# Layer 1's own rows scattered in rank order at layer 0's end, layer 3's masks built in batch norm's stage, and three chunks' sums on ScalarE

## The chip, the cores and the metric

The kernel runs on one core of one Trainium2 chip. The metric is the device time of one execution in microseconds (us). The program computes four layers of a small graph network in one launch. A core has five engines that work through queues of their own: PE (TensorE, the matrix array), DVE (VectorE), ACT (ScalarE), POOL (GpSimd) and SP (SyncE, which in this kernel only issues transfers). Semaphores order them against each other. POOL also issues all transfers whose addresses come from an index in memory (gathers and scatters)[...].

## The reference

There are N = 2708 nodes with D = 128 features, and an adjacency matrix `adj` of 2708 x 2708 floats that is stored densely but has about 17 non-zeros in a row, the diagonal always among them. Each layer is wrapped in the same way:

```python
x = _layernorm(x + layer(x, adj), axis=-1)      # four times
# layer 0
msg = H.T @ X ; msg * (1 / H.sum(axis=0))[:, None]
# layer 1
s = x @ msg_w[:, :D].T ; d = x @ msg_w[:, D:].T
messages = gelu(s[:, None, :] + d[None, :, :] + msg_b)
aggregated = einsum('ijd,ij->id', messages, adj)
h = gelu(concatenate([x, aggregated]) @ upd_w.T + upd_b) + x ; layernorm(h)
# layer 2
h = A @ (x @ W) + b ; batch norm of h over the nodes ; leaky relu, 0.2
# layer 3, for each of 4 heads
E = leaky_relu((x @ w1)[:, None, :] + (x @ w2)[None, :, :], 0.01)
s = exp(tanh(E @ a / 8) * 8) * A ; s = s / s.sum(-1)
out = leaky_relu(s @ x @ Wlin.T, 0.01)           # then the four heads side by side @ w
```

Layers 1 and 3 need the messages only where `adj` is not zero, so the kernel first finds each row's non-zeros.

## The kernel before

**Blocks and ranks.** The nodes are handled in 22 blocks (21 of 128 nodes and one of 20). The blocks form two groups, `GROUPS` = (0, 13), (13, 22), split at `SPLIT` = 13. Within each group the nodes get a `rank` by their number of non-zeros, largest first, and from layer 1 on a block means 128 nodes that are neighbours in rank. So all rows of a block have nearly the same count, and block b needs only `CAPS[b]` messages per row (30 down to 8). `perm` holds for each rank the node's own number, `idx` the numbers of its neighbours, `ls` their weights.

**Layer 0 and the search (0 to about 205 us).** SP loads row blocks of `adj` through a ring of nine buffers (L388). For each block, `count_and_sum` lets PE add the block's part of `adj.T @ x` and of the column sums to PSUM (L405), POOL clears the diagonal (L395) and ScalarE counts the row's non-zeros with a Sign over the whole row (L416). `extract` (L420 to L471) is VectorE's search: the eight largest of each of 11 segments of 247 columns with their places, then the 32 largest of these as two sets of keys, one for the value and one for the place. `ranking(g)` (L478 to L504) sends the counts of a group to all partitions by way of DRAM and lets ScalarE count, with one Sign for each block (L502), how many keys lie above; `ranked(g)` turns the count into `rank`. `lists` (L514 to L543) decodes the keys on VectorE into weights and column numbers, and `place` scatters each row's list on POOL to its rank in `lists_dram`; `sorted_lists` (L558) reads the table back in rank order into `ls`, `idx` and `perm`. In this stage only the first group, blocks 0 to 12, is searched; group 1's ranking is issued after layer 0's last block, and its search takes place inside layer 1. The order of VectorE's instructions here is that of the program; the other engines' queues are ordered by a scheduler from the program's dependencies.

**Layer 0's end (175 to 205 us).** `layer0` (L722 to L783) is a generator that normalises up to four blocks at once: the sum and residual on VectorE, Squares and a root on ScalarE, the scaling on VectorE into `xs`, a transposition and the product with `wd_t` on PE (that is d), a copy on ScalarE. Both halves go to `dx_dram` in node order through SP: d in the row's first 512 bytes, x in the second. Six of these generators run staggered (L785 to L795). The weights that PE needs transposed come in through `weight` (L369), whose load ScalarE issues and whose transposition is at the front of PE's queue.

**Layer 1 with layer 2 (205 to 840 us).** A loop over the 22 rank blocks in the order `TURNS`. For a block, `own_row` gathers its own 1-KB rows (d and x) from `dx_dram` by `perm` on POOL into one of three buffers `x_s`, one block ahead (L808). `messages` computes s on PE, then gathers chunks of up to eight neighbours' d, one gather of 128 rows of 512 bytes for each neighbour place, into five buffers `msg` (L816; `dx_dram` is seen as a table of 2N half rows, hence the factor 2 in `idx`); VectorE adds s, ScalarE takes gelu, VectorE weighs and sums. Beside it, two at most of the row blocks are loaded again and transposed through PE into `at_dram` (`transposed`, L898), and group 1's search is done. `update` (L860) makes the new x of the block, scatters it, and keeps x @ W. From the twelfth block on, `layer2(k)` (L942) gathers 128 rows of `at_dram` at a time (1.35 MB) on POOL into the same ring and multiplies them on PE (L949) while layer 1 still runs.

**Batch norm (840 to 905 us).** Statistics over the nodes, the normalised x, its products with the second weights of layer 3 (the rows of `t2_dram`), and scatters of x by rank.

**Layer 3 (905 to 1610 us).** The nodes of each group are cut once more, into 24 blocks of `BLOCKS3`: a block takes g rows in each quarter of the partitions with up to 128 // g neighbours each, and consists of chunks of four rows each; 100 chunks in all. `masks(g)` (L1164) builds for each of the seven values of g, on first use, constant 0/1 matrices that copy, sum and pick rows; it is called inside `prepare`, step by step, while the preceding block is at work. The order of PE, VectorE and ScalarE is that of the program here. For each chunk: `fetch` gathers the neighbours' four parts from `t2_dram` on POOL into one of nine buffers; `repeated` (L1275) copies x1 to the neighbours' partitions on PE, into z3 (three rows) and z1 (one row, where PE adds the neighbours' part too, L1288); VectorE adds z3 to the gathered rows (L1483). Then the score of each row and head, a sum over 128 numbers, is done in one of two ways: `scores` (L1294) does product and sum on VectorE, four instructions a row, and `products` (L1303) with `sums_of_products` (L1310) does the product of two rows in one VectorE instruction and the sums in eight ScalarE instructions. Of each chunk's four rows, two take the first way and two the second. `rest` and `finish` (L1319, L1368) do tanh, exp, the weights, the products with the neighbours' x (L1360), the heads' linear maps (`al`, `lin` at L1386), the last product and the normalisation; `step` queues their pieces between the chunks' instructions. A dense version of the last two layers behind a flag is not run with these inputs.

Of the kernel before, what the change touches and what calls it, by code (L numbers as in the profile page):

```python
# [9 lines left out]
FP = mybir.dt.float32  # L10
AF = mybir.ActivationFunctionType
ALU = mybir.AluOpType
# [73 lines left out]
def gnn_resnorm_kernel(  # L86
# [124 lines left out]

    dx_dram = tables.tile([NBLK * P, 2 * D], FP, name="dx_dram")
# [30 lines left out]
    def gather(dst, table, index, rows=N):  # L243
        nc.gpsimd.indirect_dma_start(  # L244
            out=dst,
            out_offset=None,
            in_=table[0:rows, :],
            in_offset=bass.IndirectOffsetOnAxis(ap=index, axis=0),
        )
# [84 lines left out]
    with ExitStack() as layer:  # L334
# [22 lines left out]
        nc.gpsimd.iota(places_i, pattern=[[-256, CAND]], base=256 * CAND, channel_multiplier=0)  # L357
# [11 lines left out]
        def weight(src, name):  # L369
            raw = small.tile([P, P], FP, name="raw_w")  # L370
            nc.scalar.dma_start(raw, src)
# [142 lines left out]
        def lists(b0, b1):  # L514
# [8 lines left out]
            nc.vector.tensor_copy(rows[:, :, 2 * SLOTS], cnt[:, b0:b1])  # L523
            nc.vector.tensor_copy(rows[:, :, 2 * SLOTS + 1], node[:, b0:b1])
            nc.vector.tensor_copy(rows[:, :, 0], diag[:, b0:b1])
            nc.vector.tensor_copy(rows[:, :, SLOTS], node[:, b0:b1])
            nc.vector.tensor_copy(code, k2[:, b0:b1, 0 : SLOTS - 1])
            nc.vector.tensor_scalar(low, code, 255, None, ALU.bitwise_and)
            nc.vector.tensor_scalar(seg, code, 8, None, ALU.arith_shift_right)
            nc.vector.tensor_scalar(seg, seg, -1.0, float(CAND), ALU.mult, ALU.add)  # L530
            nc.vector.tensor_scalar(seg, seg, 3, None, ALU.arith_shift_right)
            nc.vector.tensor_scalar(seg, seg, float(NSEG - 1), 0.0, ALU.min, ALU.max)
            cols = rows[:, :, SLOTS + 1 : 2 * SLOTS]
            nc.vector.scalar_tensor_tensor(cols, seg, float(SEGW), low, ALU.mult, ALU.add)
            nc.vector.tensor_scalar(cols, cols, float(N - 1), 0.0, ALU.min, ALU.max)
            nc.vector.scalar_tensor_tensor(cols, v1, 0.0, cols, ALU.is_gt, ALU.mult)
            nc.vector.tensor_scalar(
                seg, seg, float(SPAN), float(127 - TOP), ALU.mult, ALU.add
# [19 lines left out]
        def sorted_lists(g):  # L558
# [3 lines left out]
            for c0, c1, n in parts:  # L562
# [6 lines left out]
                nc.vector.tensor_scalar(  # L569
                    idx[0:n, c0:c1, :], ls[0:n, c0:c1, SLOTS : 2 * SLOTS], 2.0, None, ALU.mult  # L570
                )
# [150 lines left out]
        def layer0(b0, count, n):  # L722
# [31 lines left out]
            nc.vector.reciprocal(v, v)  # L754
            for j in range(count):
                nc.vector.tensor_scalar(
                    xs[0:n, b0 + j, :], h[0:n, j, :], sums[:, j : j + 1], v[:, j : j + 1],
# [3 lines left out]
            nc.sync.dma_start(  # L761
                dx_dram[b0 * P : b0 * P + w, D : 2 * D].rearrange("(b p) w -> p b w", p=n),
# [1259 lines left out]
```

## Time and profile before

| | |
|---|---|
| time, median of 3 runs | 1965.46 us |
| the three runs | 1963.5, 1975.81, 1965.46 us |
| the profiled execution | 1612.16 us |
| its span on the core | 1610.4 us |
| its mean TensorE clock | 0.708 of full speed |
| PE, PE weight loads | 1170.0, 827.4 us (73%, 51%) |
| VectorE, ScalarE, POOL | 1182.0, 697.6, 897.8 us (73%, 43%, 56%) |
| moved by DMA | 288.21 MB, mean 179 GB/s |
| message gathers (L244), 368 | 349.7 us, 950 ns each |
| layer 3's gathers (L244), 400 | 403.6 us, 1009 ns each |
| ScalarE's sums (L1314), 800 | 235.2 us, 295 ns each |
| VectorE's scores (L1298), 400 of each kind | 91.7 us, 284 ns each (z1's row) |
| VectorE's products (L1306), 100 | 121.1 us, 1211 ns each |
| VectorE's sum with z3 (L1483), 100 | 174.8 us, 1748 ns each |

The profile covers one execution. Its span is the time from the first to the last instruction on the core; busy times are of that span. A row of the profile names line, engine, operation and the tiles it writes and reads; "idle before" is the engine's idle time ahead of such an instruction, with what ended it. PE's clock is the share of full speed that the chip granted. The profiled execution is far shorter than the timed runs, so times taken from it are compared with each other and not with the median.

### The profile page before, as it was taken

Reading aid. Unit: us, or ns where it says so; the run is one execution under the profiler, and the core shown is the slowest. Engines: PE = TensorE matmul, PEld = TensorE weight load, DVE = VectorE, ACT = ScalarE, POOL = GpSimd, SP = SyncE. Lnnn points to the kernel's source line nnn. Section 1 sums busy time; section 2 is a strip of 40 time slices with the busy share of each in tenths; the row PEclk is TensorE's granted clock in tenths of the full one; section 3 lists DMA queues with packets and bytes.
Section 4 is the critical chain, followed back from the end, with each engine's and each line's share of the span. In section 5 each row is a group of like instructions: output and inputs, shape, how many; then the busy total and the mean of one; then the engine's idle time right before and its main releaser. Section 6 shows DMA issues by size and latency. Waiting matters only on the chain. (4 is left out here: it accounts for less than half of the span.)

```text
span 1610.4 us, 23528 instructions
## 1 busy us (share of the span) xinstructions
PE 1170.0 (73%) x5771; PEld 827.4 (51%) x5771; DVE 1182.0 (73%) x5376; ACT 697.6 (43%) x2670; POOL 897.8 (56%) x996
## 2 busy tenths in 40 slices
PE   6996333555357536666896689988888988998994
PEld 6896323344246435565783234544554545555553
DVE  7999967888356554444547398897888888888883
ACT  3448467655235311111115244544444555455442
POOL 1001167777667577765613577665656656676521
PEclk9898655655556677677678766776787778767675
DMA  8733368888358734343333779875766766877630
GB/s 273 286 141 127 94 186 201 246 248 237 101 136 215 224 77 164 128 169 140 104 109 121 245 229 225 234 223 159 221 204 198 209 187 166 230 199 215 186 92 8
DMA packets 164685, 288.21 MB, mean 179 GB/s; under 512 B 46610, under 2 KB 118512, under 8 KB 157439
## 3 DMA queue, kind: packets, MB, share of 16 engines
q0 software_dynamic: 60496, 190.76, 40.9%
q1 hardware_dynamic: 95923, 90.91, 18.1%
q10 hardware_dynamic: 8120, 4.95, 1.2%
q8 instruction: 48, 0.79, 0.2%
q14 instruction: 98, 0.80, 0.2%
HBM read 242.50 MB, written 43.97 MB: 178 GB/s over the span
## 5 line engine op out<-in xcount | busy, mean ns | idle before, releaser
L244 POOL DMA_INDIRECT g<-t_dram,idx x400 | 403.6, 1009 | 189.3 <-issue 141.1
L244 POOL DMA_INDIRECT msg<-dx_dram,idx x368 | 349.7, 950 | 119.1 <-issue 93.9
L1314 ACT ACTIVATE sum_junk<-g 126x128 bf16<-126x128 f32 (+3 forms) x800 | 235.2, 295 | 115.8 <-DVE g L1306 63.4
L1283 PE MATMUL z<-x,copies 32*126 32x512 f32 (+3 forms) x800 | 210.8, 875 | 33.1 <-DVE g L1483 32.3
L949 PE MATMUL acc<-x_nat,at_rows 128*128 128x128 f32 (+2 forms) x968 | 151.0, 319 | 83.1 <-DMA at_rows<-at_dram,perm 82.7
L923 PE MATMUL pt_a<-ident,rows 128*128 128x128 f32 (+2 forms) x475 | 110.1, 388 | 133.6 <-ACT at_sb L928 132.3
L949 PEld LDWEIGHTS acc<-x_nat,at_rows 128*128 128x128 f32 (+2 forms) x968 | 138.0, 226 | 93.2 <-DMA at_rows<-at_dram,perm 75.9
L1483 DVE TENSOR_TENSOR g<-g,z 126x1536 f32<-126x1536 f32 (+3 forms) x100 | 174.8, 1748 | 11.7 <-PE z L1283 11.2
L1288 PE MATMUL z<-g,ident 126*126 126x512 f32 (+3 forms) x200 | 164.7, 918 | 0.0
L923 PEld LDWEIGHTS pt_a<-ident,rows 128*128 128x128 f32 (+2 forms) x475 | 80.2, 200 | 156.4 <-ACT at_sb L928 152.6
L1314 ACT ACTIVATION_READ_ACCUMULATOR sum_junk<-g 126x1 f32 (+3 forms) x800 | 149.5, 187 | 0.0
L835 DVE SCALAR_TENSOR_TENSOR own<-msg,ls,own 128x128 f32<-128x128 f32 (+1 forms) x302 | 105.4, 349 | 56.1 <-ACT msg L853 53.5
L1360 PEld LDWEIGHTS po_s<-wm,g 126*128 126x128 f32 (+3 forms) x800 | 118.6, 232 | 42.1 <-DVE wm L1347 32.7
L1360 PE MATMUL po_s<-wm,g 126*128 126x24 f32 (+6 forms) x800 | 120.5, 305 | 25.0 <-DVE wm L1347 23.3
L405 PE MATMUL acc<-x_nat,rows 128*128 128x129 f32 (+3 forms) x1012 | 130.5, 291 | 11.2 <-DMA rows<-in_adj_dram 11.2
L405 PEld LDWEIGHTS acc<-x_nat,rows 128*128 128x128 f32 (+2 forms) x1012 | 125.2, 201 | 16.2 <-DMA rows<-in_adj_dram 11.7
L1306 DVE SCALAR_TENSOR_TENSOR g<-g,a_ps 126x1024 f32<-126x1024 f32 (+3 forms) x100 | 121.1, 1211 | 0.0
L435 DVE MAX8 cv<-rows 128x8 f32<-128x247 f32 (+2 forms) x242 | 95.5, 400 | 6.7 <-POOL rows L395 6.7
L1288 PEld LDWEIGHTS z<-g,ident 126*126 126x126 f32 (+3 forms) x200 | 40.6, 254 | 116.3 <-issue 89.7
L1283 PEld LDWEIGHTS z<-x,copies 32*126 32x126 f32 (+3 forms) x800 | 63.7, 239 | 70.6 <-DVE g L1483 27.0
L430 DVE FIND_INDEX8 ci<-cv,rows 128x8 uint32<-128x247 f32 (+2 forms) x242 | 98.4, 407 | 0.0
L1298 DVE SCALAR_TENSOR_TENSOR g<-z,a 126x128 f32<-126x128 f32 (+3 forms) x400 | 91.7, 284 | 2.3 <-PE z L1288 0.9
(297 smaller groups left out, 2093.2 us busy)
## 6 DMA issues: line engine op xcount, KB each, us to landing
rows<-in_adj_dram SPq DMA_DIRECT2D x34, 1354.0 KB
at_dram<-at_sb SPq DMA_DIRECT2D x105, 256.0 KB
g<-t_dram,idx POOLq DMA_INDIRECT x400
msg<-dx_dram,idx POOLq DMA_INDIRECT x368
t_dram<-t_row SPq DMA_DIRECT2D x21, 256.0 KB
at_dram<-at_sb SPq DMA_DIRECT2D x21, 64.0 KB
dx_dram<-x_nat SPq DMA_DIRECT2D x5, 256.0 KB
dx_dram<-d_sb SPq DMA_DIRECT2D x5, 256.0 KB
```

The source lines that it names most:

```text
L244: nc.gpsimd.indirect_dma_start(out=dst, out_offset=None, in_=table[0:rows, :], in_offset=bass.IndirectOffsetOnAxis(ap=index, axis=0),)
L405: nc.tensor.matmul(accs0[k][0:m, c0 : c0 + f1 - f0], lhsT=rows[0:n, j0 : j0 + m], rhs=x_nat[0:n, b, f0:f1], start=k not in started, stop=( ...
L430: nc.vector.max_index(out=ci[0:n, at], in_max=cv[0:n, at], in_values=rows[0:n, c0 : c0 + cw])
L835: nc.vector.scalar_tensor_tensor(to, m, v, last, ALU.mult, ALU.add)
L923: nc.tensor.transpose(pt[0:m, j, 0:n], rows[0:n, c0 : c0 + m], ident[0:n, 0:n])
L949: nc.tensor.matmul(accs2[ib // 4][0:m, (ib % 4) * D : (ib % 4 + 1) * D], lhsT=at[0:n, i0 : i0 + m], rhs=xw[0:n, b, :], start=(k == 0 and i ...
L1283: nc.tensor.matmul(z3[0:e, r, :] if r < 3 else z1[0:e], lhsT=copies[g][rows, j, :], rhs=own[b][1][rows, :], start=True, stop=r < 3, skip_g ...
L1288: nc.tensor.matmul(z1[0:e], lhsT=ident[0:e, 0:e], rhs=g4[0:e, 3, 0:HD], start=False, stop=True, skip_group_check=True,)
L1306: nc.vector.scalar_tensor_tensor(z, z, 0.0, a_ps[0:e].unsqueeze(1).to_broadcast((e, 2, HD)), ALU.max, ALU.mult)
L1314: nc.scalar.activation(junk[0:e], g4[0:e, r, hd * D : (hd + 1) * D], AF.Identity, accum_out=sc[0:e, r, hd : hd + 1],)
L1360: nc.tensor.matmul(po[:, p0 * HEADS : (p0 + g) * HEADS], lhsT=g4s[i][0:e, r, HD : HD + D], rhs=wm[0:e, 4 * i + r, :, :], start=True, stop= ...
L1483: nc.vector.tensor_tensor(z, z, z3[0:e], ALU.add)
```

## The change

It has six pieces.

- **The tables of layer 0's end.** d gets a table of its own, `d_dram`, in node order, so that the messages' gathers read rows of it by the node's number without the factor 2. d and x of a block lie side by side in a new tile `dx`, and POOL scatters each block's 1-KB rows to their rank in `dx_dram`: 22 scatters.
- **Own rows.** `own_row` becomes a plain load of 128 neighbouring rows of `dx_dram` on SP's queue, in place of the gather on POOL.
- **The ranking of group 1** has to be there before its blocks are scattered: it is issued ahead of layer 0's loop, and `ranked(1)` comes after the first loop instead of inside layer 1. Blocks from the 13th on wait in their generator until then.
- **Weights and lists.** `weight` loads on SP's queue instead of ScalarE's. `lists` decodes the segment in three operations fewer on VectorE, and four of its copies go to ScalarE.
- **Masks.** `masks` is no longer a generator and moves to batch norm's stage: the kinds 4, 5 and 6 ahead of the loop that normalises, the other four behind it. The results live in a pool of their own, `ready`.
- **Three rows' sums.** In every even chunk of a block of layer 3, three rows instead of two take the way over `products` and ScalarE's sums, and VectorE's four `scores` for the third row are left out. Odd chunks stay as they were.

The diff, cut to its core:

```diff
+    d_dram = tables.tile([NBLK * P, D], FP, name="d_dram")
     dx_dram = tables.tile([NBLK * P, 2 * D], FP, name="dx_dram")
...
-        nc.gpsimd.iota(places_i, pattern=[[-256, CAND]], base=256 * CAND, channel_multiplier=0)
+        nc.gpsimd.iota(places_i, pattern=[[-256, CAND]], base=256 * (CAND + 7), channel_multiplier=0)
...
             raw = small.tile([P, P], FP, name="raw_w")
-            nc.scalar.dma_start(raw, src)
+            nc.sync.dma_start(raw, src)
...
-            nc.vector.tensor_copy(rows[:, :, 2 * SLOTS], cnt[:, b0:b1])
-            nc.vector.tensor_copy(rows[:, :, 2 * SLOTS + 1], node[:, b0:b1])
-            nc.vector.tensor_copy(rows[:, :, 0], diag[:, b0:b1])
-            nc.vector.tensor_copy(rows[:, :, SLOTS], node[:, b0:b1])
+            for at, of in ((0, diag), (SLOTS, node), (2 * SLOTS, cnt), (2 * SLOTS + 1, node)):
+                nc.scalar.copy(rows[:, :, at], of[:, b0:b1])
...
-            nc.vector.tensor_scalar(seg, code, 8, None, ALU.arith_shift_right)
-            nc.vector.tensor_scalar(seg, seg, -1.0, float(CAND), ALU.mult, ALU.add)
-            nc.vector.tensor_scalar(seg, seg, 3, None, ALU.arith_shift_right)
-            nc.vector.tensor_scalar(seg, seg, float(NSEG - 1), 0.0, ALU.min, ALU.max)
+            nc.vector.tensor_scalar(seg, code, 11, None, ALU.arith_shift_right)
...
-                nc.vector.tensor_scalar(
-                    idx[0:n, c0:c1, :], ls[0:n, c0:c1, SLOTS : 2 * SLOTS], 2.0, None, ALU.mult
-                )
+                nc.vector.tensor_copy(idx[0:n, c0:c1, :], ls[0:n, c0:c1, SLOTS : 2 * SLOTS])
...
+            dx = brief.tile([P, count, 2, D], FP, name=f"dx{count}", bufs=3 if count > 1 else 2)
...
-            d_sb = brief.tile([P, 4, D], FP, name="d_sb")
-            nc.scalar.copy(d_sb[0:n, 0:count], pm[0:n, 0:count])
+            nc.scalar.copy(dx[0:n, :, 0, :], pm[0:n, 0:count])
             nc.sync.dma_start(
-                dx_dram[b0 * P : b0 * P + w, 0:D].rearrange("(b p) w -> p b w", p=n),
-                d_sb[0:n, 0:count],
-            )
+                d_dram[b0 * P : b0 * P + w, :].rearrange("(b p) w -> p b w", p=n),
+                dx[0:n, :, 0, :],
+            )
+            while b0 + count > SPLIT and 1 not in known:
+                yield
+            for j in range(count):
+                did = scatter(
+                    dx_dram, rank[0:n, b0 + j : b0 + j + 1],
+                    dx[0:n, j].rearrange("p t d -> p (t d)"),
+                )
...
+        known = [0]
         running = []
+        ranking(1)
         for quad in [(NFULL, 1, NREM), *quads()[:-1]]:
...
+        ranked(1)
+        known[0] = 1
         while running:
...
         sorted_lists(0)
-        ranking(1)
...
-            gather(
-                x_s[0:n].rearrange("p t d -> p (t d)"), dx_dram, perm[0:n, b : b + 1]
+            nc.sync.dma_start(
+                x_s[0:n],
+                dx_dram[b * P : b * P + n, :].rearrange("p (t d) -> p t d", t=2),
             )
...
-                    gather(
-                        msg[0:n, k, :], dx_dram.rearrange("n (t d) -> (n t) d", t=2),
-                        idx[0:n, b, c0 + k + 1 : c0 + k + 2], rows=2 * N,
-                    )
+                    gather(msg[0:n, k, :], d_dram, idx[0:n, b, c0 + k + 1 : c0 + k + 2])
...
-                    if e == SPLIT:
-                        ranked(1)
...
+        for g in KINDS[:3]:
+            masks(g)
         for b0, count, n in quads():
...
+        for g in KINDS[3:]:
+            masks(g)
...
-        def products(e, g4):
+        def products(e, g4, count):
...
-            for r in range(2):
+            for r in range(count):
...
-            if BLOCKS3[b][0] not in copies:
-                yield from masks(BLOCKS3[b][0])
-                yield
...
-            products(e, g4)
+            count = 2 if j % 2 else 3
+            products(e, g4, count)
             step()
-            sums_of_products(e, g4, sc4)
-            scores(e, 2, g4[:, 2, 0:HD], a_ps, g4, sc4[:, 2, :])
+            sums_of_products(e, g4, sc4, count)
+            if count == 2:
+                scores(e, 2, g4[:, 2, 0:HD], a_ps, g4, sc4[:, 2, :])
```

## The prediction

> **What bounds the kernel now.** I read the stretches first: busy time of each engine, cut where the stages change (columns: stretch, its length, then busy us and instruction count of PE, weight loads, DVE, ACT, POOL, then TensorE clock, DMA share, GB/s).
>
> ```profile
> 0.00:175.00 175.00, 131.04 (x1017) 125.52 (x1017) 163.92 (x884) 82.36 (x79) 20.84 (x89) 0.90 0.54 192
> 175.00:210.00 35.00, 19.02 (x105) 15.58 (x105) 28.73 (x177) 21.66 (x75) 5.89 (x7) 0.70 0.55 150
> 300.00:400.00 100.00, 56.33 (x247) 44.65 (x247) 83.50 (x445) 56.33 (x114) 73.96 (x78) 0.60 0.85 244
> 600.00:700.00 100.00, 64.25 (x401) 57.97 (x402) 45.26 (x175) 16.43 (x40) 75.37 (x80) 0.70 0.46 163
> 840.00:905.00 65.00, 41.41 (x198) 26.89 (x198) 37.84 (x155) 31.23 (x89) 22.69 (x25) 0.87 0.50 156
> 1025.00:1125.00 100.00, 88.36 (x359) 51.02 (x361) 84.91 (x354) 47.60 (x280) 63.12 (x65) 0.70 0.68 197
> ```
>
> Layer 0's search is VectorE's (164 of 175 us). In layer 1 no engine looks full, but 80 POOL instructions in 100 us are one each 1.25 us, and POOL's timeline shows that this is its pace (start, duration, engine, line, what, and the idle time before with its releaser):
>
> ```profile
> 205.45 0.99 POOL L244 DMA_INDIRECT x_s<-dx_dram,perm  x1 [27.58 <-ACT junk L502]
> 206.74 0.95 POOL L244 DMA_INDIRECT x_s<-dx_dram,perm  x1 [0.30 <-issue]
> 208.00 0.95 POOL L244 DMA_INDIRECT msg<-dx_dram,idx  x1 [0.31 <-issue]
> 209.25 0.95 POOL L244 DMA_INDIRECT msg<-dx_dram,idx  x1 [0.30 <-issue]
> ...
> 717.39 0.92 POOL L244 DMA_INDIRECT x_s<-dx_dram,perm  x1 [8.29 <-issue]
> 747.19 0.95 POOL L244 DMA_INDIRECT x_s<-dx_dram,perm  x1 [7.42 <-issue]
> 772.53 0.94 POOL L244 DMA_INDIRECT x_s<-dx_dram,perm  x1 [9.64 <-issue]
> ```
>
> From 205.45 to 831.4 POOL issues 443 instructions; at 1.255 us they fill 556 of 626 us. So POOL sets layer 1 and most of layer 2. Of the 70 us of longer gaps, 31 stand before four own-row gathers (6.6, 8.3, 7.4, 9.6), which wait for a block's update to free one of three x_s buffers, and hold up the message and at_rows gathers behind them. Layer 3 (100 chunks, 6.6 us each) is tight on PE (585 of 650 us, 925 to 1575) and DVE (563) together; their waits there:
>
> ```profile
> PE z L1283 <- DVE g L1483: 32.3, 42, 2.2
> PE po_s L1360 <- DVE wm L1347: 22.4, 22, 1.2
> DVE inv L1344 <- PE few_ps L1400: 34.3, 20, 4.9
> DVE lin_s L1388 <- ACT lin_s L1386: 18.8, 20, 1.6
> ACT lin_s L1386 <- PE pl_s L1381: 32.7, 21, 2.2
> ```
>
> PE waits some 55 us for DVE, DVE some 55 us for PE: a saving on either is passed on only in part. The very start shows a needless wait: PE's first instruction transposes a weight and waits for its load, and all matmuls, POOL's clearing of the diagonal and the search stand behind it:
>
> ```profile
> 15.21 0.45 PE L373 MATMUL pt_w<-ident,raw_w 128*128 128x128 f32 x1 [15.21 <-DMA raw_w<-in_L_gnn_msg_w_dram]
> 16.49 0.74 DVE L435 MAX8 cv<-rows 128x8 f32<-128x247 f32 x2 [6.70 <-POOL rows L395]
> ```
>
> **What the Trainium skill says.** Perfetto Trace Analysis, section DMA Instruction — SWDGE (GPSIMD): a GpSimd DMA's slice is descriptor generation and not the data's movement. The trace agrees: slices keep 0.95 us for 512-byte and for 1-KB rows, so what counts of a moved gather is its slot of 1.25 us. DMA: Bandwidth & Descriptors, section Anatomy of one DMA, gives about 2 us of fixed time, mostly completion. Here the last lists scatter starts at 176.90, its slice ends at 177.86, and the load that waits for it goes out at 179.12. TensorE: Matmul & The Clock Gate, section What's actually happening, says that the array runs at half rate until kept busy; the trace has the same pair of matmuls (L1111) at 2.05 and 1.10 us. Perfetto Trace Analysis, section Optimizing Scalar/DVE Operations, advises moving work to ScalarE when VectorE is saturated; true here only as far as ScalarE is not waited for.
>
> **Part 1, layer 0.** The weights' transposes leave the front of PE's order (the changed order has row matmuls first). The search can start when DVE is free (9.8) and the first rows are there; that arrival is not shown. Bounds: 0 to 6.7 us; I take 5.5. Each list call loses three DVE operations (0.15 to 0.3 us each) and four copies (0.07): about 2 us for the two calls here. So VectorE's part ends 7.5 us earlier. But the four copies go to ScalarE, where those of the last list wait for the buffer that the second batch of list scatters frees: last six scatters from 163, 6 x 1.265, landing 1.3: about 172 instead of ScalarE's 175.24 before. Gain 3 us.
>
> **Part 2, the ranking is now inside layer 0's end.** Its nine Signs (1.17 us with a pitch of 1.27, L502) alternate with layer 0's squares, which ScalarE did without them: 11.4 us. Before, the first d copy ended 13.3 us after the first square (175.24 to 188.56); now 13.3 + 11.4 after 172, so 196.5. Queued behind the Signs on ScalarE: every sqrt, so DVE's normalisation, the transposes and d. Three reads of whole rows (2.46 us each) come between too, but behind the point that matters.
>
> **Part 3, 22 scatters.** From 196.5 POOL issues 22 x 1.255 = 27.6 us, to 224; the later ones wait for rank (ready near 192 to 204) and for buffers that the first free (three tiles), which this pace covers. The messages' gathers stand behind them: first message slot at 224 against a first own-row slot at 205.45: **+18.6 us** (+12 to +25). The own-row load on SP waits for the last scatter (226.5) and holds behind it at_dram stores, so transposes; these are needed first at 543, which hides some 20 us; without that cover, they would add it.
>
> **Part 4, layer 1.** 22 own-row gathers leave POOL: 22 x 1.255 = **-27.6 us**. As SP loads they cost 0.4 us each on a queue that is mostly idle. Of the 31 us of gaps before four of them I credit half, **-15** (0 to -31): afterwards PE's two at_rows blocks and one update (2 x 6.2 + 8 us at the clock of that stretch) are late next. The doubling of the index becomes a copy, and message rows keep 512 bytes: nothing.
>
> **Part 5, batch norm.** Masks of 4, 5 and 6 rows stand on DVE ahead of the first normalised block: eight, six and five copies of 0.21, sums of 1.8, 1.4 and 1.15, and 0.6 of small ones: 10.1 us. DVE is idle there for 3.9 (until ps_v) and 0.8 us, so **+5.4** (0 to +10): the matmuls of t2's rows, which set the rest, start so much later. The other four (8.6 us) lie beside those matmuls, and 14 iotas on POOL ahead of or between the x3 scatters (0.15 to 0.27 each) in its idle time; without that cover 3 us. At layer 3's start the 4.2 us of the first mask fall away, of which the weights' copies keep 0.8: **-3.4**.
>
> **Part 6, layer 3.** The masks of the other kinds were 14.6 us of DVE. Three chunks' sums: on 56 even chunks DVE loses four scores (0.205 pitch, 0.82) and its product grows from 1024 to 1536 (1.13 to 1.66): -0.29 each, 16 us. ScalarE gains four sums of 0.29, 1.16 us, and starts 0.53 later, so it is free 1.7 us later. What stands behind is above all lin (L1386), 22 times, in an even chunk, and DVE waits for it; it now waits some 1.5 us (32.7 / 21) for PE, so about 0.2 us each is new, 4 us, and these 22 chunks lose their gain, 6.4. Left: 14.6 + 16 - 6.4 - 4 = 20; as DVE and PE wait on each other, half: **-10** (-31 to +16, the upper end if every even chunk passes on 0.5 us).
>
> **Sum:** 18.6 - 27.6 - 15 + 5.4 - 3.4 - 10 = -32, from 1612.2 (span 1610.4 and 1.8 around) to 1580. The timed runs, 1963.5 to 1975.8, take 353 us more than the profiled one, and no view says where. I take the saving one for one: 1965.5 - 32 = **1933**; in proportion it would be 1926.
>
> **Rivals.** (a) *Slower:* layer 1 is not POOL's. If transposes and searches (DVE 83 of 100 us from 300 to 400) set it, parts 3's 18.6 stay and part 4 gives nothing: +10.6, 1976. It decides if less than 11 of part 4's 42.6 us appear. Against it: between 258 and 373 POOL has no gap over 0.4 us. (b) *ScalarE's queue bounds layer 3:* each even chunk waits 1.16 - 0.29 more, 56 x 0.87 = 49, masks -10: about +17, 1982. For it: lin is already waited for; against: ACT is busy half of the time. (c) *All passes through:* gaps 31, layer 3 31: -69, 1896. (d) *The timed runs wait for PE*, whose work is unchanged (their 353 us would fit a lower clock): only the start and a part of layer 1 remain, about -12, 1953. That own rows don't move is excluded: the changed order has 22 loads on SP and no own-row gather on POOL.
>
> **Chances.** Forecast 0.47, (a) 0.14, (b) 0.06, (c) 0.20, (d) 0.13. Range 1893 to 1975: from (c) to nearly (a). A measurement can tell about 1% (20 us) from no change: faster takes 0.85 of the forecast, (c) and a quarter of (d): 0.63; slower the upper parts of (a) and (b): 0.08; the rest 0.29.
>
> **What would show it.** First search near 11, not 16.5; first message gather near 224, POOL without gaps before own rows; layer 2's end near 816 instead of 840; layer 3's DVE waits on lin above 19 us but under 30. Wrong if the gathers start after 235, if layer 2 ends after 835, or if layer 3 takes longer than its 705 us.

## The result, and the profile after

The changed kernel takes 1956.42 us (median of 15 runs, 1937.29 to 1965.62), the kernel before 1972.69 us beside it (15 runs). The ratio is 0.9895, with a 95% interval of 0.9869 to 0.9920: 21 us faster, between 16 and 26. The forecast was 32 us faster, 1933.

These two lines of the page of the changed kernel stand first (span, then busy time of each engine with its share and its instructions):

```profile
span 1956.3 us, 23628 instructions
...
PE 1248.6 (64%) x5771; PEld 866.9 (44%) x5771; DVE 1173.2 (60%) x4900; ACT 768.6 (39%) x3134; POOL 896.4 (46%) x996
```

VectorE has 476 instructions less than before, ScalarE 464 more, POOL as many as before. But the span is 346 us longer than that of the profiled execution of before. The timed kernels of before were as long as this one all along (1963 to 1982 us); it was the profiled execution, 1610 us, that stood apart. The comparison runs below were made on four chips: on two of them the kernel before takes 1622 and 1624 us, on two others 1977 and 1945. By its time, the profile from which the forecast was worked out belongs to the first sort, and the timed runs to the second; their own chips are not on record. Each chip was used in one group of runs only, so it is not shown whether the chip itself makes the sort or something else that held while that group ran.

The kernel before, profiled once more on a chip of the second sort, shows part of where the 377 us lie. From its page and from its list of waits (engine and line, releaser: total us, times, longest):

```profile
span 1987.0 us, 23528 instructions
...
PE 1287.3 (65%) x5771; PEld 898.0 (45%) x5771; DVE 1190.7 (60%) x5376; ACT 699.5 (35%) x2670; POOL 894.1 (45%) x996
```

```profile
ACT lin_s L1386 <- remote: 46.3, 8, 7.7
...
DVE val L617 <- remote: 42.2, 6, 14.5
...
PE z L1283 <- issue: 38.9, 14, 14.2
...
DVE g L1483 <- remote: 28.8, 5, 10.2
```

VectorE, ScalarE and POOL work as long as before within 1% (1190.7 against 1182.0, 699.5 against 697.6, 894.1 against 897.8), PE 117 us longer at a clock of 0.653 instead of 0.708. The packets of the gathers' and scatters' queue took as much of the DMA engines' time as before, too (33.5% of 1987 us against 40.9% of 1610). New are waits for which the profile names no releaser ("remote", "issue"): summed over its list, VectorE waits 257 us in this way and ScalarE 362, where the profile of the first sort has 0 and 54. What these waits are, and how much of the 377 us is theirs and how much PE's, stays open.

So the changed kernel's trace can be set against that of before only from a chip of the same sort. These are the milestones of five executions, read from the timelines (first search, first message gather on POOL, last at_rows matmul, start of the first and of the last addition of z3, end, in us):

| | search | message | layer 2's end | layer 3 from, to | span |
|---|---|---|---|---|---|
| before, chip of 1620 (the profile above) | 16.5 | 208.0 | 839.6 | 920.6, 1570.3 | 1610.4 |
| changed, chip of 1620 | 12.0 | 231.5 | 835.1 | 916.6, 1567.0 | 1607.6 |
| before, chip of 1970 | 16.6 | 210.8 | 1056.8 | 1151.0, 1947.7 | 1987.0 |
| before with the new start, same chip | 12.1 | 207.4 | 1040.4 | 1136.7, 1918.6 | 1957.8 |
| changed, chip of 1970 | 12.0 | 229.8 | 1052.9 | 1145.2, 1914.7 | 1956.3 |

Each line is one execution. The two of the chips of 1620 differ by 3 us, while the medians of the two kernels there differ by 19: that of before is some 10 us shorter than the medians of its kernel (1622 and 1624), that of the changed kernel 4 us longer than its own (1605). So this pair shows where time went, but not all of the gain.

The start of the messages on POOL's timeline of the changed kernel (start, duration, engine, line, what, and the idle time before with its releaser):

```profile
170.59 0.96 POOL L253 DMA_INDIRECT lists_dram<-lists,rank  x1 [0.30 <-issue]
197.29 0.96 POOL L253 DMA_INDIRECT dx_dram<-dx,rank  x1 [25.74 <-ACT dx L773]
...
215.79 0.96 POOL L253 DMA_INDIRECT dx_dram<-dx,rank  x1 [2.28 <-ACT dx L773]
...
225.93 0.96 POOL L253 DMA_INDIRECT dx_dram<-dx,rank  x1 [0.30 <-issue]
229.77 0.99 POOL L245 DMA_INDIRECT msg<-d_dram,idx  x1 [2.88 <-DVE cv L436]
...
292.35 0.94 POOL L245 DMA_INDIRECT msg<-d_dram,idx  x1 [16.45 <-issue]
```

The scatters run from 197.3 to 226.9, one each 1.27 us, and the messages follow at 229.8. The last line is what the forecast did not have: with no own-row gather left in its queue, POOL still stands idle for 16 us ahead of a block's messages. In POOL's timeline of the kernel before, a gap of 13 us opens at about the same place, and two gaps of 5 and 11 us around the next own rows (same columns, chip of 1970):

```profile
279.89 0.94 POOL L244 DMA_INDIRECT msg<-dx_dram,idx  x1 [13.17 <-issue]
...
312.56 0.94 POOL L244 DMA_INDIRECT x_s<-dx_dram,perm  x1 [5.26 <-DVE cv L435]
...
324.64 0.94 POOL L244 DMA_INDIRECT msg<-dx_dram,idx  x1 [11.14 <-ACT at_sb L928]
```

### The profile page after: what moved, and what is told of

It reads as the page before. It is cut to its first block, busy times and chain, and to the rows that moved or that the text cites. A ratio compares the mean times of both kernels' runs of the same rounds, so it can differ in the third digit from the quotient of the medians.

```text
span 1956.3 us, 23628 instructions
## 1 busy us (share of the span) xinstructions
PE 1248.6 (64%) x5771; PEld 866.9 (44%) x5771; DVE 1173.2 (60%) x4900; ACT 768.6 (39%) x3134; POOL 896.4 (46%) x996
## 5 line engine op out<-in xcount | busy, mean ns | idle before, releaser
L245 POOL DMA_INDIRECT msg<-d_dram,idx x368 | 348.7, 947 | 272.1 <-issue 225.7
L1324 ACT ACTIVATE sum_junk<-g 126x128 bf16<-126x128 f32 (+3 forms) x1024 | 302.6, 298 | 142.3 <-issue 60.8
L1293 PE MATMUL z<-x,copies 32*126 32x512 f32 (+3 forms) x800 | 220.3, 917 | 60.7 <-DVE g L1490 33.9
L957 PE MATMUL acc<-x_nat,at_rows 128*128 128x128 f32 (+2 forms) x968 | 168.8, 335 | 64.5 <-issue 52.6
L931 PE MATMUL pt_a<-ident,rows 128*128 128x128 f32 (+2 forms) x475 | 119.0, 408 | 131.5 <-ACT at_sb L936 106.9
L1324 ACT ACTIVATION_READ_ACCUMULATOR sum_junk<-g 126x1 f32 (+3 forms) x1024 | 193.5, 189 | 0.0
L957 PEld LDWEIGHTS acc<-x_nat,at_rows 128*128 128x128 f32 (+2 forms) x968 | 151.2, 240 | 78.8 <-issue 67.5
L1370 PE MATMUL po_s<-wm,g 126*128 126x24 f32 (+6 forms) x800 | 124.7, 310 | 59.7 <-DVE wm L1357 53.8
L931 PEld LDWEIGHTS pt_a<-ident,rows 128*128 128x128 f32 (+2 forms) x475 | 86.4, 212 | 154.8 <-ACT at_sb L936 120.9
L1316 DVE SCALAR_TENSOR_TENSOR g<-g,a_ps 126x1536 f32<-126x1536 f32 (+6 forms) x100 | 151.1, 1511 | 0.0
```

What stands on the lines that cost most here:

```text
L245: nc.gpsimd.indirect_dma_start(out=dst, out_offset=None, in_=table[0:N, :], in_offset=bass.IndirectOffsetOnAxis(ap=index, axis=0),)
L931: nc.tensor.transpose(pt[0:m, j, 0:n], rows[0:n, c0 : c0 + m], ident[0:n, 0:n])
L957: nc.tensor.matmul(accs2[ib // 4][0:m, (ib % 4) * D : (ib % 4 + 1) * D], lhsT=at[0:n, i0 : i0 + m], rhs=xw[0:n, b, :], start=(k == 0 and i ...
L1293: nc.tensor.matmul(z3[0:e, r, :] if r < 3 else z1[0:e], lhsT=copies[g][rows, j, :], rhs=own[b][1][rows, :], start=True, stop=r < 3, skip_g ...
L1316: nc.vector.scalar_tensor_tensor(z, z, 0.0, a_ps[0:e].unsqueeze(1).to_broadcast((e, count, HD)), ALU.max, ALU.mult)
L1324: nc.scalar.activation(junk[0:e], g4[0:e, r, hd * D : (hd + 1) * D], AF.Identity, accum_out=sc[0:e, r, hd : hd + 1],)
```

## The experiments

Twelve runs, all but the first timed in rounds against the kernel before on their own chip; differences in us are the ratio's distance from 1 times the median of before there. They ran in four groups: the first four on a chip where before takes 1977 us, the next four on one of 1622, then two on one of 1624 and two on one of 1945. In what follows "1620" and "1970" stand for the two sorts; what is said of a sort was measured on one or two chips of it.

**The kernel before, unchanged**, for a trace from a chip of the second sort.

> The kernel before, unchanged, for a second trace of it. The changed kernel's profiled execution (1956.3 us of span) lies at its timed runs, that of before (1610.4 us) far under its own. If that one was an odd execution, this one has a span near 1965 us, a mean TensorE clock near 0.67 instead of 0.708, and layer 1 with layer 2 takes some 820 us instead of 635, with idle times of 10 us and more ahead of many message gathers on POOL. If the profiled execution of before is what this kernel does, the span is near 1610 us again and the changed kernel lost 340 us that the timed comparison does not show, which I think impossible.

It took 1988.88 us, its span was 1987.0 at a clock of 0.653, and the first message to the last at_rows matmul took 846 us: the forecast's profile of before was the odd one beside the timed runs. Its trace is the one shown above.

**Own rows alone.** The changed tables, scatters, ranking, own rows and indices; weights, lists and layer 3 as before.

```diff
+        ranking(1)
         for quad in [(NFULL, 1, NREM), *quads()[:-1]]:
...
+                did = scatter(dx_dram, rank[0:n, b0 + j : b0 + j + 1], ...)
...
-            gather(x_s[0:n].rearrange("p t d -> p (t d)"), dx_dram, perm[0:n, b : b + 1])
+            nc.sync.dma_start(x_s[0:n], dx_dram[b * P : b * P + n, :]...)
```

> Before, with the own rows' piece alone: the tables of layer 0's end, 22 scatters by rank, group 1's ranking ahead of layer 0's loop, own rows loaded by SP, indices not doubled. My theory (POOL paces layer 1): +21 at the start of the messages (+18.6, and the weights' start not gained), -27.6 for the gathers, -15 for gaps, so -20 to -24 us, ratio near 0.989. Rival A (POOL does not pace layer 1 in the timed executions, since the changed kernel's POOL is idle for 10 to 17 us ahead of a block's messages some fifteen times): what the later start adds stays and nothing comes back, +10 to +20 us, ratio 1.005 to 1.01. Rival B: the three x_s buffers paced it, filled by POOL or by SP alike: about 0 to +20.

The ratio is 1.0015 (0.9995 to 1.0036): +3 us, not clear of no change. On this chip the theory of the forecast falls: the piece does not gain 20. The trace shows both sides of it. The first message goes out at 233.8 instead of 210.8, 23 us later; from there to POOL's last scatter it takes 808 us, against 840, 827 and 830 in the three traces of the same chip that have the old own rows.

**Start and lists alone.**

```diff
-            nc.scalar.dma_start(raw, src)
+            nc.sync.dma_start(raw, src)
...
+            for at, of in ((0, diag), (SLOTS, node), (2 * SLOTS, cnt), (2 * SLOTS + 1, node)):
+                nc.scalar.copy(rows[:, :, at], of[:, b0:b1])
```

> Before, with the weights' loads on SP and the shorter decoding of the lists alone. My theory: the search starts 5.5 us earlier and VectorE loses 2 us; layer 0's end waits for the lists' copies on ScalarE, so -3 to -7 us, ratio 0.9965 to 0.9985. Rival: the ring's loads set the search's pace in the timed executions, and the start gives nothing: 0 within 2 us.

0.9966 (0.9943 to 0.9988), -7 us. The first search starts at 12.1 instead of 16.6, and the first message at 207.4 instead of 210.8: the start passes to the messages almost whole.

**Masks and three rows' sums**, layer 3's two pieces.

```diff
+        for g in KINDS[:3]:
+            masks(g)
...
-            products(e, g4)
+            count = 2 if j % 2 else 3
+            products(e, g4, count)
```

> Before, with layer 3's two pieces alone: masks in batch norm's stage and three rows' sums on ScalarE in even chunks. My theory: +5.4 in batch norm, -3.4 at layer 3's start, -10 in its body, so -8 us, ratio 0.996 (range -30 to +16). Rival A, which has the whole gain of the change come from here: -20 us or more, ratio under 0.990. Rival B, ScalarE's queue bounds the even chunks: +17 us, ratio 1.009.

0.9871 (0.9838 to 0.9905), -25 us: rival A's number, three times the forecast. From the first to the last z3 addition layer 3 takes 773 us, against 797, 793 and 782 in the three traces of this chip with the old layer 3.

**Masks alone** (the first two lines of that edit), now on the chip of 1622 us.

> Before, with the masks built in batch norm's stage and the sums left as they were. Together with the sums this gave -25 us. By my sum: +5.4 in batch norm, -3.4 at layer 3's start, half of 14.6 in its body: -5 us, ratio 0.997. If layer 3 passes VectorE's savings on whole and the masks cost batch norm nothing, as the trace of both pieces together suggests (batch norm to the first z 89.5 us against 90.8), it is -18 us, ratio 0.991. If the sums alone bring it, 0 within 3 us.

0.9927 (0.9896 to 0.9957), -12 us. Batch norm's stage takes them for nothing, as its stretches show (length, then PE, weight loads, VectorE, ScalarE, POOL: busy us and instructions, then TensorE clock, DMA share, GB/s), first before, then with the masks:

```profile
840.00:917.00 77.00, 45.83 (x207) 28.97 (x207) 43.76 (x174) 32.08 (x91) 31.95 (x34) 0.81 0.57 176
```

```profile
841.00:919.00 78.00, 46.84 (x208) 29.52 (x208) 55.40 (x239) 32.42 (x91) 29.13 (x39) 0.80 0.48 147
```

VectorE works 11.6 us more, and from the end of layer 2 to the first z3 addition it takes 81.6 us instead of 81.0. The forecast had +2 for this (5.4 in batch norm less 3.4 at layer 3's start). From its first to its last z3 addition layer 3 takes 641.4 us in this trace, against 649.7 and 658.1 in the two traces of such chips with the old layer 3 (before, and own rows by SP below).

**Three rows' sums alone** (the last three lines), twice.

> Before, with three rows' sums on ScalarE in even chunks and the masks left in layer 3. By my sum: VectorE saves 16 us, 10 of them are given back at lin, half of the rest passes: -3 us, ratio 0.9985. If layer 3 passes VectorE's savings on whole: -16 us, ratio 0.992. If ScalarE's queue bounds the even chunks: +20 us, ratio 1.010. With e4, the two should add to -25.

> Three rows' sums on ScalarE in even chunks alone, beside the run above. On a chip of 1620 us: +8 us as measured there, ratio 1.005. On a chip of 1970 us masks and sums together gave -25: if the masks bring the 12 us there that they brought on the other chip, the sums are -13 us, ratio 0.993; if the sums cost 8 us there too, the masks would have to bring 33, more than the 18 us of VectorE's work that they remove, and the ratio is 1.004.

1.0049 (1.0029 to 1.0068) on the chip of 1622, 1.0021 (1.0003 to 1.0040) on that of 1624: 8 and 3 us slower. Layer 3's stretch, first before, then with the sums on the chip of 1622 (columns as above):

```profile
917.00:1570.00 653.00, 587.52 (x2434) 332.67 (x2434) 563.07 (x2343) 322.82 (x1889) 415.79 (x421) 0.73 0.70 200
```

```profile
924.00:1579.00 655.00, 585.61 (x2434) 329.03 (x2435) 546.52 (x1896) 385.09 (x2327) 414.28 (x420) 0.74 0.72 199
```

VectorE saves 16.6 us, as worked out, and in this trace nothing comes of it: it waits these 16.6 us and 2 more. A part of them shows in its waits of that stretch:

```profile
DVE lin_s L1388 <- ACT lin_s L1386: 27.7, 21, 1.5
DVE inv L1344 <- PE few_ps L1400: 24.8, 16, 5.1
DVE al L1255 <- PE few_ps L1339: 20.1, 11, 3.7
...
DVE g L1298 <- PE z L1288: 7.0, 21, 0.4
```

Before, these four were 18.8, 34.3, 11.1 and 0.9 us. The wait for lin grew by 9 us, which the forecast put at 4; VectorE also waits longer for PE at al and at z1's row, and 9.5 us less at inv; PE is busy 90% of the stretch before (587.5 of 653). (The title and part 6 of the forecast say "three chunks' sums"; what moved are the sums of three rows in a chunk.)

**The change without own rows.**

> The changed kernel without the own rows' piece: the start, the lists, the masks and the sums. If the pieces add up, -6.7 and -25 make -32 us against before, ratio 0.984, some 10 us below the changed kernel. If the own rows' piece gives more beside the others than alone (where it cost 3 us), it is at or above the changed kernel's 0.9895.

0.9966 (0.9950 to 0.9982) on the chip of 1622: -5 us. The start, the masks and the sums together give little on this chip: of the masks' 12 us the sums take back 8, which leaves some 2 us for the start.

**Own rows by SP, with no scatter by rank.** Each block gets the own rows of 128 neighbouring nodes instead of those of its rank; sizes and instructions are kept. It takes POOL's 22 gathers away and adds nothing ahead of the messages.

```diff
-            gather(x_s[0:n].rearrange("p t d -> p (t d)"), dx_dram, perm[0:n, b : b + 1])
+            nc.sync.dma_start(x_s[0:n], dx_dram[b * P : b * P + n, :].rearrange("p (t d) -> p t d", t=2))
```

> Before, with own rows loaded by SP as 128 neighbouring rows of the table in node order: no scatter by rank, no earlier ranking. What it leaves out is the order: a block gets other nodes' own rows, so the output is not the reference's, while each instruction keeps its size. POOL loses 22 gathers and nothing is added ahead of the messages. My theory of layer 1 (POOL's slots pace it): -27.6 for the slots and -15 for gaps, -43 us, ratio 0.978. If POOL's slots are hidden in the timed executions and the own rows' piece costs 3 us because both sides of it are hidden: 0 within 5 us. If the 23 us of later start count in full and the gathers were worth about 20: -20 us, ratio 0.990.

0.9902 (0.9865 to 0.9939), -16 us, on the chip of 1622. That is well under the 43 of the forecast's step, on the very sort of chip that it was worked out for, and it was measured without a later start in the way.

**The whole change once more**, on the chip of 1624 us.

> The whole change once more, beside the kernel before. The chips on which these calls ran differ: 1977 us for the kernel before on one, 1622 on the other. On a chip of 1970 us the pieces add to -28 (start -6.7, own rows +3, layer 3's two -25) and -20.7 was measured: ratio 0.988 to 0.991. On a chip of 1620 us the same kernel without the own rows' piece stood at 0.9966, and own rows by SP without the scatters at -15 us; if the scatters' later start (+19 to +23) counts in full there, own rows give +4 to +8 and the whole change -1.5 to +3 us, ratio 0.999 to 1.002. If my theory of layer 1 held on such a chip (POOL's slots set the pace, -43 against +19), it would be 0.982.

0.9880 (0.9851 to 0.9910): -19 us, outside what I had expected from adding the pieces (-1.5 to +3), and outside the forecast's 32 too. Against the change without own rows (-5, on another chip of the same sort) the own rows are worth 14 us here, 8 to 20 by the two intervals.

**The change with two rows' sums in every chunk.**

```diff
-            count = 2 if j % 2 else 3
+            count = 2
```

> The changed kernel with two rows' sums on ScalarE in every chunk, as before the change: start, lists, own rows and masks stay. On a chip of 1620 us the sums alone cost 3 and 8 us in two measurements, and the whole change stood at 0.988: if that holds inside the whole too, this is 0.983 to 0.986 and beats both kernels. On a chip of 1970 us the whole stood at 0.9895, and masks with sums gave -25: if the sums were half of these 25 there, this is 0.995; if they cost there too, it is 0.986.

0.9953 (0.9931 to 0.9975) on the chip of 1945 us: -9 us. The whole change stood at -21 on a chip of its sort. So on these chips three rows' sums would be worth 12 us (5 to 18), where on the others they cost 3 to 8. That is a difference of two ratios from two chips, and the traces do not confirm it. Layer 3's stretch with masks alone, then with masks and sums (the changed kernel; columns as above):

```profile
1123.00:1881.00 758.00, 619.58 (x2433) 345.90 (x2433) 551.10 (x2273) 323.78 (x1888) 418.74 (x416) 0.70 0.62 175
```

```profile
1142.00:1914.00 772.00, 623.31 (x2434) 347.58 (x2435) 535.42 (x1833) 390.51 (x2328) 418.23 (x416) 0.69 0.61 172
```

The stretch without the sums is the shorter one. But its chip is 1.4% faster, and its execution is 14 us under the median of its runs, so the two traces don't settle it either.

**Messages late**: before, with 22 more gathers of 512-byte rows on POOL, into buffers that nobody reads.

```diff
+        for k in range(NBLK):
+            late = mine.tile([P, D], FP, name="late", bufs=10)
+            gather(late, dx_dram.rearrange("n (t d) -> (n t) d", t=2),
+                   idx[:, 0, k + 1 : k + 2], rows=2 * N)
         ahead = own_row(0)
```

> Before, with 22 more gathers of 512-byte rows on POOL ahead of the first own rows, into buffers that nobody reads: the messages start 22 slots, 27.6 us, later, and nothing else of layer 1 is changed. If POOL's slots set layer 1's pace (my step of 18.6 us for the later start), it is +27.6 us, ratio 1.017 on a chip of 1620 us and 1.014 on one of 1970. If layer 1's length is set by the other work, which goes on meanwhile (on a chip of 1620 us own rows by SP without the later start gave -15 and the piece with it -14), it is +0 to +5 us, ratio 1.000 to 1.003. On a chip of 1970 us own rows with the later start cost 3 us: +5 to +25 if the slots were worth as much as on the other.

1.0128 (1.0090 to 1.0166) on the chip of 1945: +25 us. POOL's timeline shows that the added gathers lie ahead of all else, and that the first message goes out at 236.3 (208 to 211 without them):

```profile
232.53 0.94 POOL L244 DMA_INDIRECT late<-dx_dram,idx  x1 [0.30 <-issue]
233.77 0.95 POOL L244 DMA_INDIRECT x_s<-dx_dram,perm  x1 [0.30 <-issue]
235.02 0.95 POOL L244 DMA_INDIRECT x_s<-dx_dram,perm  x1 [0.30 <-issue]
236.27 0.94 POOL L244 DMA_INDIRECT msg<-dx_dram,idx  x1 [0.30 <-issue]
```

So on this sort of chip a later start of the messages is paid for about in full (18 to 32 us by the interval), and own rows, which start 23 us later and cost 3, gain about 20 in layer 1 (worked out, not measured alone there). On the chips of 1620 the same sum gives 2 us for the later start (14 against 16 without it, uncertain by 8); that was not measured alone.

The pieces side by side, in us, with the forecast's terms (a dash where it was not run; "by difference" from two of the ratios above):

| | forecast | chips of 1620 | chips of 1970 |
|---|---|---|---|
| start and lists | -3 | -2 by difference | -7 |
| own rows | -21 | -14 by difference | +3 |
| masks | -5 | -12 | -14 or -5 by difference |
| three rows' sums | -3 | +8, +3 | -12 by difference |
| the whole change | -32 | -19 | -21 |

The forecast's own rows are parts 2 to 4: 18.6 with the 3 us of the start taken out again, 21.6, less 27.6 and 15. Masks and sums are parts 5 and 6, with the 10 us of the body shared by what VectorE saves there. For the masks on the chips of 1970, -14 is masks with sums (-25) without the sums' 12, and -5 is the change with two rows' sums (-9) without start and own rows. What was measured there directly, -7, +3 and -25, adds to -29 where the whole gave -21; the intervals allow for that. No kernel here is shown to beat the changed one on both sorts of chip. By these numbers the change with two rows' sums should be the best on those of 1620 and the change without own rows on those of 1970; neither was run there.

## Why the forecast was right in its sum and wrong in its parts

The direction and the size, 21 us where 32 were forecast, came out within the stated range. But the mechanism held only in part, and part of the agreement is luck: terms that were wrong cancelled, and differently on the two sorts of chip.

**Layer 0's end (parts 1 to 3): right.** First search near 11 was forecast, 12.0 measured; the lists' copies on ScalarE at 172, 172.97 measured; the first scatter at 196.5, 197.29 measured; 22 slots of 1.255 us, 1.27 measured. Two small waits were missed: 2.3 us within the scatters for the last d, and 2.9 us (7.1 on the chip of 1624) between the last scatter and the first message. So the messages start at 229.8 and 231.5 instead of 224, still short of the 235 that I had named as the limit. That this start counts in full was right on the chip of 1970 where it was tried (+25 us for 25.5 later). On the chips of 1620, for which it was worked out, own rows give 16 us without the scatters ahead and 14 with them, so a start 23 us later costs some 2 us there, uncertain by 8.

**The gaps of part 4: the step that failed.** "Of the 31 us of gaps before four of them I credit half, -15." These 15 us did not come. POOL's queue from the first message to its last scatter, all idle times over 0.45 us in it summed from the timelines:

| | length | slots | idle | ahead of own rows | ahead of messages | ahead of x's scatters |
|---|---|---|---|---|---|---|
| before, 1620 | 624 | 441 | 75 | 33 | 9 | 24 |
| changed, 1620 | 596 | 421 | 72 | 0 | 18 | 51 |
| own rows by SP, no scatters, 1620 | 615 | 421 | 94 | 0 | 32 | 49 |
| before with the new start, 1970 | 827 | 441 | 288 | 136 | 88 | 59 |
| changed, 1970 | 816 | 421 | 297 | 0 | 162 | 131 |

Twenty slots fewer are 25 us. (Two of the 22 own rows stood ahead of the first message.) The idle time of the changed kernel is that of before on both sorts of chip: it has moved from the own rows to the messages behind them and to the scatters of x. The own row was only the first instruction in POOL's queue to find the block's update unfinished; the next one finds it unfinished as well. The scatters of x with the three longest waits ahead of them show it on the chips of 1620 (POOL's timeline, before and changed):

```profile
553.03 1.00 POOL L252 DMA_INDIRECT x_dram<-x_n,perm  x1 [4.79 <-DVE x_n L318]
...
818.26 0.99 POOL L252 DMA_INDIRECT x_dram<-x_n,perm  x1 [6.98 <-DVE x_n L318]
...
831.40 0.97 POOL L252 DMA_INDIRECT x_dram<-x_n,perm  x1 [12.16 <-DVE x_n L318]
```

```profile
572.71 1.00 POOL L253 DMA_INDIRECT x_dram<-x_n,perm  x1 [16.97 <-DVE x_n L319]
...
808.84 1.00 POOL L253 DMA_INDIRECT x_dram<-x_n,perm  x1 [11.88 <-DVE own L846]
...
826.58 0.97 POOL L253 DMA_INDIRECT x_dram<-x_n,perm  x1 [16.74 <-DVE x_n L319]
```

At 572.71 POOL waits 17 us for one x_n; before, the 6.7 us ahead of an own row and 4.8 us ahead of x's scatter stood there.

Without the scatters ahead, the idle time even grows: the five traces of the chips of 1620 with the old own rows have 624 to 631 us of length and 75 to 83 of idle time, so that only 9 to 16 of the 25 us of slots come back. This fits the 16 us of the runs, and it means that on these chips neither the slots nor the later start count in full: the forecast's -43 is -16, and its +22 some +2.

With the gaps at nothing and the rest as forecast, own rows come to about +22 - 27.6 = -6 us. By the traces of the chips of 1620 layer 2's end lies 4.5 us earlier than in the forecast's profile, the start's share included, and 4 to 11 us earlier than in the five traces with the old own rows (839.6 to 846.4). It was forecast at 816 and named wrong from 835 on; it is 835.1. By the runs the piece is worth 14 us there, and nothing or -3 on the chips of 1970. The sum of -6 lies between these two, but why they differ is open.

**"POOL sets layer 1 and most of layer 2": half right.** On the chips of 1620 POOL's slots fill 549 of 624 us (those other than the 75 idle). On those of 1970, where the times of this case were taken, POOL is idle for 288 of 827. The engines that a block's turn passes through wait longer there: over the whole span, VectorE's listed waits add up to 762 us against 392 in the forecast's profile.

**Part 5: right.** Masks in batch norm cost nothing net in the trace, 0.6 us against the +2 forecast.

**Part 6: right in its sum for the chips of the profile, but not in its halves, and too small for the chips of the times.** Half of VectorE's savings was to pass. By the traces of the chips of 1620 the masks pass on some 8 of their 13.6 us (layer 3 from 649.7 to 641.4), and the sums none of theirs; with both, layer 3 takes 650.4 us, as long as before. The runs there have -12 for the masks and +3 to +8 for the sums, -4 to -9 together, where the forecast had -5 and -3. On the chip of 1970, masks and sums shorten VectorE's work from 565.6 to 535.3 us, and layer 3 from 782, 793 or 797 to 773: 9 to 24 of the 30 us pass. By the runs, layer 3's two pieces give -25 there where the forecast had -8, which made up for what own rows did not give. In the two stretches (columns as above; first before, then with masks and sums) PE is busy 81 and 80% of the time, not 90:

```profile
1147.00:1947.00 800.00, 651.95 (x2433) 369.64 (x2433) 565.63 (x2339) 324.19 (x1887) 415.15 (x421) 0.66 0.57 163
```

```profile
1135.00:1911.00 776.00, 621.68 (x2436) 349.77 (x2434) 535.25 (x1832) 389.76 (x2326) 418.24 (x417) 0.70 0.60 171
```

That PE's spare time is what lets VectorE's savings pass would fit, but it was only argued: no run changed PE's work. The two lines show a rival. With as many matmuls, PE's busy time falls by 30 us in the second, at a clock of 0.70 instead of 0.66, and the stretch by 24. The timed runs have a higher clock with these pieces too (0.671 on average against 0.661; the whole change on the chip of 1624, 0.718 against 0.700). Whether that clock is a cause or a result was not tested. It is not the whole account, as the sums alone had a higher clock as well (0.705 against 0.700) and were slower.

Perfetto Trace Analysis, section Optimizing Scalar/DVE Operations, in the Trainium skill says that offloading work to ScalarE may make sense when VectorE is saturated. On the chips of 1620, with VectorE busy 86% of layer 3, the move cost 3 to 8 us; on those of 1970 it gained 12, by difference.

**The rivals.** (a), layer 1 not paced by POOL, was named with +10.6 for the whole change and is nearest to what own rows did on the chips of 1970 (+3 alone); it did not show in the sum, since layer 3 gave more than forecast there. (b) is part of the truth on the chips of 1620: the wait for lin grew to 28 us, within the 19 to 30 forecast, and the sums lose there. (d), a lower clock in the timed runs, had the lower clock right (0.653 for the kernel before, against 0.708 in the profile) and the conclusion wrong: it left 12 us of the change, and layer 3's pieces alone gave 25 there.

**The step from 1612 to 1965 us,** "no view says where. I take the saving one for one", is the weakest of the working: the two numbers belong to different sorts of chip. It held for the sum (-19 us on one sort, -21 on the other), but own rows went from 14 us of gain to none, and the sums from a loss to a gain, as far as differences between runs tell.

## What to carry to other kernels

An idle time ahead of an instruction belongs to what it waits for, not to the instruction: before crediting its removal, look for the next instruction in that queue which needs the same thing, as it will inherit the wait. And when a profiled execution and the timed runs differ by a fifth, settle first whether they come from the same conditions; a sum can come out right while its terms cancel.

Slots taken out of a queue come back only as far as nothing else is late, and slots put ahead of its first use cost only as far as nothing else would have been late: here 25 us on one chip and some 2, uncertain by 8, on others.

## What the runs showed of the hardware

The same program takes 1622 and 1624 us on two chips and 1977 and 1945 on two others, with the same busy time on VectorE, ScalarE and POOL within 1% in the two profiles of it. In its runs on the sort of 1970 the clock of PE is lower (0.65 to 0.67 against 0.69 to 0.72), and in its profile VectorE and ScalarE have, added up, some 560 us of waits more for which no releaser is named. One move of work, three rows' sums to ScalarE, costs 3 to 8 us on the first sort; that it gains on the second rests on a difference between two chips.

A gather or scatter of POOL takes a slot of 1.25 to 1.29 us in its queue, of which some 0.95 us are its own duration, for rows of 512 bytes and of 1 KB alike.
